# Layer 1 of a four-layer network on one core: turning onto token partitions with 128 columns of identity, and an MLP that begins with one step's statistics

## The chip, the cores and the metric

The kernel runs on one core of one Trainium2 chip. A core has a matrix engine (PE, or TensorE) with a separate path that loads its stationary operand (PEld), a vector engine (DVE), an activation engine (ACT), a general engine (POOL) and a sync engine (SP) that here issues all the data transfers. The metric is the device time of one execution in microseconds (us); lower is better. The time before is the median of three runs.

## The reference

The network works on `x` of shape 4 x 96 x 64 x 64 (batch, channels, height, width), so on 4 x 4096 = 16,384 tokens of 96 channels, in float32. Layer 0 is a two-block Mamba with a batch norm, layer 1 a ConvNeXt block, layers 2 and 3 attention-like and Fourier mixing with small quantized MLPs. The change touches layer 1 alone:

```python
def _L1_conv_ref(x, conv_w, conv_b, ln_g, ln_b, w1, b1, w2, b2, layer_scale):
    h = depthwise_conv(x, conv_w, 7 x 7, padding 3) + conv_b      # each channel by itself
    h = jnp.transpose(h, (0, 2, 3, 1))
    mu = jnp.mean(h, axis=-1, keepdims=True)                      # over the 96 channels
    var = jnp.var(h, axis=-1, keepdims=True)
    h = (h - mu) * jax.lax.rsqrt(var + LN_EPS) * ln_g + ln_b
    h = jax.nn.gelu(jnp.einsum('bhwc,cf->bhwf', h, w1) + b1, approximate=False)   # 96 -> 384
    h = jnp.einsum('bhwf,fc->bhwc', h, w2) + b2                                   # 384 -> 96
    h = jnp.transpose(h, (0, 3, 1, 2)) * layer_scale[None]
    return h + x
```

## The kernel before, in words

Layers run one after another. Layer 0 takes the first 2605 us and leaves its result in device memory (`scratch`); layer 1 is the function `layer1`; layers 2 and 3 follow. Inside layer 1, PE, DVE, ACT and POOL run their instructions in the order in which the program text issues them (`tc.manual_schedule`); the transfers on SP's queue are placed among each other by a planner, which works from its own estimate of when each is needed.

Layer 1 has three stages.

**The turn.** The tokens are cut into 16 chunks of 1024 (4 images x 4). For each chunk, `tokens` loads 96 x 1024 values of layer 0's output (`o`, 384 KB) and of the residual (`xr`, 384 KB), each with three buffers; ACT applies layer 0's batch norm to `o` (line 736), DVE adds `xr` and writes the sum into the resident tile `t` (line 737), which holds channels on the partitions. `turn` then transposes the chunk onto partitions of 128 tokens each: eight matmuls (line 744), with a block of 96 channels x 128 tokens of `t` as stationary operand and the identity as moving operand, four of them into one PSUM tile `xt_ps` of 128 x 4 x 96 (four buffers). ACT copies the first half of a chunk out (line 750), DVE the second (line 748), into the tile `xt`. In program order `tokens` of the next chunk stands ahead of `turn` of this one.

**The convolution.** With 128 tokens (two image rows) on the partitions, the 7 x 7 convolution of one channel is four matmuls with banded 128 x 128 matrices over 128 columns (lines 787 and 790). Channels go in 24 groups of 4; a group's matrices (`band`, 1 MB) are loaded with three buffers (line 761). For the fourth matmul POOL makes a copy with halves swapped (`outer`, lines 768 and 769), two groups at a time. Ahead of the ninth group, `consts2` prepares the weights of the later layers: many small loads, and a chain of small operations that ends in matmuls on PE (line 703).

**The MLP.** The 32 blocks of 512 tokens go in 8 steps of 4. Each step `k` has its statistics: `stats(k, d)` is 4 pairs of DVE operations (lines 810 and 811), and `roots(k)` turns the 16 variances into reciprocal roots by a logarithm and an exponential on ACT (lines 815 and 816). For each block `i`, `back(i)` normalizes (DVE, line 824), transposes back by identity matmuls (PE, line 829, 4 x 128 columns) and copies out (DVE, line 831); `hidden(i)` is three matmuls of 512 columns (line 838) with an exact GELU each on ACT (line 839); `out(i)` is three more matmuls (line 844) and a DVE addition into `t` (line 847). The logarithm and the exponential need other tables on ACT than the GELU, so that going over costs a table load each way. Before the first `hidden`, the kernel does the statistics and roots of steps 0 and 1 and the four `back` of step 0. After that, `back` runs four blocks ahead of `hidden`, the statistics two steps ahead, and `roots(k + 2)` stands at the end of step `k`.

A float32 matmul appears in the trace as two instruction records, each with its weight load.

Of the kernel before, what the change touches and what calls it, by code (L numbers as in the profile page):

```python
# [9 lines left out]
F32 = mybir.dt.float32  # L10
# [8 lines left out]
B, C, HW, L = 4, 96, 64, 4096  # L19
# [8 lines left out]
ACT_EXP_LN = "natural_log_exp_and_others"  # L28
# [22 lines left out]
class Net:  # L51
# [661 lines left out]
    def layer1(self, scratch, t):  # L713
        tc, nc, ins = self.tc, self.nc, self.ins
# [3 lines left out]
        with ExitStack() as ctx:  # L718
            xpool = ctx.enter_context(tc.tile_pool(name="l1x", bufs=1))
            xt = xpool.tile([128, C, B, NR + 4], F32, name="xt")  # L720
            cb = xpool.tile([128, C], F32, name="cb")
            nc.sync.dma_start(cb, ins["c_b_row"].partition_broadcast(128))
            with (
                tc.manual_schedule(engines=engines),
                tc.tile_pool(name="l1a", bufs=1) as wk,
                tc.tile_pool(name="l1ap", bufs=1, space=PSUM) as psum,
            ):
                for at in (slice(0, 2), slice(NR + 2, NR + 4)):
                    nc.gpsimd.memset(xt[:, :, :, at], 0.0)
                def tokens(b, s):  # L730
                    at = slice(b * L + s * T, b * L + (s + 1) * T)
                    o = wk.tile([C, T], F32, name="o", tag="o", bufs=3)
                    nc.sync.dma_start(o, scratch[:, at])
                    xr = wk.tile([C, T], F32, name="xr", tag="xr", bufs=3)
                    nc.sync.dma_start(xr, ins["x"][b, :, s * T : (s + 1) * T])
                    nc.scalar.activation(o, o, AF.Identity, scale=self.osc, bias=self.osh)
                    nc.vector.tensor_add(t[:, at], o, xr)

                def turn(b, s):
                    for h in range(2):  # L740
                        ps = psum.tile([128, 4, C], F32, name="xt_ps", tag="xt", bufs=4)
                        for d in range(4):
                            a = b * L + s * T + (4 * h + d) * 128
                            nc.tensor.matmul(ps[:, d], t[:, a : a + 128], self.ident[:C, :C], start=True, stop=True)
                        r = 2 + s * (T // 128) + 4 * h
                        dst = xt[:, :, b, r : r + 4].rearrange("p c r -> p r c")
                        if h:
                            nc.vector.tensor_copy(dst, ps)
                        else:
                            nc.scalar.copy(dst, ps)  # L750

                chunks = [(b, s) for b in range(B) for s in range(NSC)]
                tokens(*chunks[0])
                for k, chunk in enumerate(chunks):
                    if k + 1 < len(chunks):
                        tokens(*chunks[k + 1])
                    turn(*chunk)

                def load(g):
                    w = wk.tile([128, GC, 4, 128], F32, name="band", tag="band", bufs=3)  # L760
                    nc.sync.dma_start(w, ins["band"][g])
                    return w

                def outer(g):

                    x2 = wk.tile([128, 2 * GC, B, NR], F32, name="x2", tag="x2", bufs=3)
                    at = slice(g * 2 * GC, (g + 1) * 2 * GC)
                    nc.gpsimd.tensor_copy(x2[:64], xt[:64, at, :, 4:])
                    nc.gpsimd.tensor_copy(x2[64:], xt[64:, at, :, :NR])
                    return x2  # L770

                def small(rows, cols):
                    ps = psum.tile([128, 4, C], F32, name="w_ps", tag="xt", bufs=4)
                    return ps.rearrange("p a c -> p (a c)")[:rows, :cols]

                x2 = [outer(0)]
                for g in range(C // GC):
                    if g == 8:
                        self.consts2(wk, small)
                    if g % 2 == 0 and g + 2 < C // GC:  # L780
                        x2.append(outer(g // 2 + 1))
                    w = load(g)
                    ps = psum.tile([128, GC, B, NR], F32, name="cv_ps", tag="cv", bufs=4)
                    for d in range(GC):
                        c = g * GC + d
                        for k, j in enumerate((1, 0, 2)):
                            nc.tensor.matmul(
                                ps[:, d], w[:, d, j], xt[:, c, :, 1 + j : 1 + j + NR], start=k == 0, stop=False
                            )
                        nc.tensor.matmul(ps[:, d], w[:, d, 3], x2[g // 2][:, g % 2 * GC + d], start=False, stop=True)  # L790
                    for d in range(GC):
                        c = g * GC + d
                        dst = xt[:, c, :, 2 : 2 + NR]
                        if g % 2:
                            nc.vector.tensor_scalar_add(dst, ps[:, d], cb[:, c : c + 1])
                        else:
                            nc.scalar.activation(dst, ps[:, d], AF.Identity, bias=cb[:, c : c + 1])

            wk = ctx.enter_context(tc.tile_pool(name="l1w", bufs=1))
            psum = ctx.enter_context(tc.tile_pool(name="l1p", bufs=1, space=PSUM))  # L800
# [3 lines left out]
            def stats(k, d):  # L804
                if d == 0:
                    mv[k] = wk.tile([128, 16, 2], F32, name="mv", tag="mv", bufs=3)
                for q in range(4 * d, 4 * d + 4):
                    b, r = divmod(16 * k + q, NR)
                    st = wk.tile([128, 6], F32, name="st", tag="st", bufs=4)
                    nc.vector.bn_stats(st, xt[:, :, b, 2 + r])  # L810
                    nc.vector.bn_aggr(mv[k][:, q], st)

            def roots(k):
                rs[k] = wk.tile([128, 16], F32, name="rs", tag="rs", bufs=3)
                nc.scalar.activation(rs[k], mv[k][:, :, 1], AF.Ln, bias=self.eps)
                nc.scalar.activation(rs[k], rs[k], AF.Exp, scale=-0.5)

            def back(i):
                k, d = divmod(i, 4)
                n = wk.tile([128, 4, C], F32, name="n", tag="n", bufs=3)  # L820
                for q in range(4):
                    b, r = divmod(4 * i + q, NR)
                    at = slice(4 * d + q, 4 * d + q + 1)
                    nc.vector.tensor_scalar(  # L824
                        n[:, q], xt[:, :, b, 2 + r], mv[k][:, at, 0], rs[k][:, at], ALU.subtract, ALU.mult
                    )
                ps = psum.tile([C, 4, 128], F32, name="tp_ps", tag="tp", bufs=2)
                for q in range(4):
                    nc.tensor.matmul(ps[:, q], n[:, q], self.ident, start=True, stop=True)
                xc[i] = wk.tile([C, MB], F32, name="xc", tag="xc", bufs=7)  # L830
                nc.vector.tensor_copy(xc[i], ps.rearrange("p r n -> p (r n)"))

            def hidden(i):
                g[i] = wk.tile([128, 3, MB], F32, name="g", tag="g", bufs=3)
                n = xc.pop(i)
                for m in range(3):
                    ps = psum.tile([128, MB], F32, name="g_ps", tag="g", bufs=4)
                    nc.tensor.matmul(ps, self.c_w1[:, m * 128 : (m + 1) * 128], n, start=True, stop=True)
                    nc.scalar.activation(g[i][:, m, :], ps, AF.Gelu, bias=self.c_b1[:, m : m + 1])
# [10 lines left out]
            n = NT // MB // 4  # L850
            with tc.manual_schedule(engines=engines):
                nc.scalar.preload_act_table_set(ACT_EXP_LN)
                for k in range(2):
                    for d in range(4):
                        stats(k, d)
                    roots(k)
                for d in range(4):
                    back(d)
                for k in range(n):
                    for d in range(4):  # L860
                        hidden(4 * k + d)
                        if k + 1 < n:
                            back(4 * k + 4 + d)
                        if k + 2 < n:
                            stats(k + 2, d)
                        if d:
                            out(4 * k + d - 1)
                    if k + 2 < n:
                        nc.scalar.preload_act_table_set(ACT_EXP_LN)
                        roots(k + 2)  # L870
                    out(4 * k + 3)
# [581 lines left out]
```

## Time and profile before

| what | value |
|---|---|
| runs | 4054.6 us median (4048.88, 4054.6, 4059.62) |
| profiled execution, its own time | 4057.1 us |
| its span, first to last instruction | 4054.9 us |
| turn: first matmul to the last copy's end | 2614.7 to 2670.5 us, 55.8 us |
| convolution: to its last copy's end | to 2793.0 us, 122.4 us |
| MLP's start: to the first `hidden` matmul | to 2818.1 us, 25.2 us |
| MLP: rest of its first step | to 2843.8 us, 25.6 us |
| MLP: the other seven steps | to 3012.0 us, 168.3 us |
| layers 2 and 3 | to 4054.9 us |
| mean granted clock of PE over the span | 0.855 of full |

In the trace, a line of the timeline gives the start and length in us, the engine, the line of the kernel, the operation, the tile written and those read, the shapes, and how many such instructions are merged; in brackets, how long the engine sat idle before and what ended that. A line of the table of windows gives a stretch, its length, busy time and number of instructions for PE, PEld, DVE, ACT and POOL, then the granted share of PE's clock, the busy share of the transfer engines and the rate in GB/s.

### The profile page before, as it was taken

How to read it: one execution, taken by the hardware profiler on the slowest of the kernel's cores; microseconds unless marked ns; L12 is line 12 of the kernel's file. 1: busy time of each engine (PE TensorE's matmuls, PEld its weight loads, DVE VectorE, ACT ScalarE, POOL GpSimd, SP SyncE). 2: the span in 40 equal slices, each digit the busy share in tenths (PEclk: the TensorE clock that was granted, in tenths of full speed). 3: DMA queues.
4: the chain of work that ended last, by engine and by line, in shares of the span. 5: the costliest groups of instructions: out<-in, count | busy, mean ns of one | idle time of the engine just before them, and what ended most of it. 6: DMA issues, size and time to landing. Idle time of an engine off the chain costs nothing. (4 is left out here: it accounts for less than half of the span.)

```text
span 4054.9 us, 45522 instructions
## 1 busy us (share of the span) xinstructions
PE 3311.5 (82%) x14174; PEld 1426.9 (35%) x14174; DVE 3193.0 (79%) x2772; ACT 2423.0 (60%) x4644; POOL 2946.8 (73%) x1571
## 2 busy tenths in 40 slices
PE   6888888888888777888888887678999887887987
PEld 3222222222222222222222221376446345556642
DVE  5999999999999999999999999724632763443649
ACT  4666667666667666666766665322445665544547
POOL 2999999999999999999999999511010455333428
PEclk8788878888878888887888887668999998889989
DMA  7667567666756666675675666363000000001111
GB/s 182 144 158 172 136 150 169 158 148 163 175 130 167 168 148 160 158 171 135 162 173 141 160 165 159 103 189 136 0 1 1 1 6 3 27 27 30 45 43 54
DMA packets 183291, 468.13 MB, mean 115 GB/s; under 512 B 53236, under 2 KB 55166, under 8 KB 179968
## 3 DMA queue, kind: packets, MB, share of 16 engines
q1 hardware_dynamic: 183048, 465.21, 46.1%
q8 instruction: 113, 1.85, 0.2%
q14 instruction: 130, 1.06, 0.1%
HBM read 391.53 MB, written 73.50 MB: 115 GB/s over the span
## 5 line engine op out<-in xcount | busy, mean ns | idle before, releaser
L496 POOL TENSOR_TENSOR hs<-hs,crep 128x1024 f32<-128x1024 f32 x768 | 1797.1, 2363 | 28.8 <-DVE hs L490 24.0
L454 PE MATMUL rep<-dbl,sel_b 32*128 32x512 f32 x1152 | 403.8, 777 | 467.8 <-DVE hs L490 441.3
L474 POOL TENSOR_TENSOR up<-udb,brep 128x1024 f32<-128x1024 f32 x256 | 604.5, 2361 | 8.5 <-DMA brep<-cd 8.5
L468 ACT ACTIVATE da<-ddb,nega 128x1024 f32<-128x1024 f32 x512 | 584.8, 1149 | 13.5 <-DVE hs L490 6.9
L468 ACT ACTIVATE dap<-ddb,nega 128x1024 f32<-128x1024 f32 x256 | 286.3, 1118 | 419.9 <-DVE hs L490 417.9
L515 PE MATMUL y<-hs,sel_r 128*32 128x512 f32 x3072 | 477.9, 693 | 4.9 <-POOL hs L496 4.9
L490 DVE TENSOR_TENSOR_SCAN hs<-da,state,rep 128x1024 f32<-128x1024 f32 x192 | 450.9, 2348 | 16.7
L490 DVE TENSOR_TENSOR_SCAN hs<-da,state,u 128x1024 f32<-128x1024 f32 x192 | 450.9, 2348 | 11.2 <-DVE u L486 1.4
L490 DVE TENSOR_TENSOR_SCAN hs<-dap,state,up 128x1024 f32<-128x1024 f32 x192 | 447.2, 2329 | 6.4 <-ACT dap L468 6.0
L210 PE MATMUL ps<-n,w_x 97*64 97x512 f32 x1536 | 376.1, 633 | 6.9 <-ACT n L323 5.4
L454 PEld LDWEIGHTS rep<-dbl,sel_b 32*128 32x128 f32 x1152 | 108.4, 216 | 766.9 <-issue 519.3
L486 DVE TENSOR_TENSOR u<-udb,rep 128x1024 f32<-128x1024 f32 x256 | 314.7, 1229 | 46.2 <-PE rep L454 15.0
L486 DVE TENSOR_TENSOR rep<-udb,rep 128x1024 f32<-128x1024 f32 x256 | 310.8, 1214 | 0.3
L1038 POOL CAST hq<-y 128x512 fp8e5<-128x512 f16 x192 | 117.7, 638 | 222.3 <-issue 136.6
L210 PEld LDWEIGHTS ps<-n,w_x 97*64 97x64 f32 x1536 | 110.6, 143 | 261.5 <-issue 215.7
L1186 POOL TENSOR_TENSOR av<-av,ec 128x780 f32<-128x780 f32 x32 | 58.8, 1837 | 197.2 <-ACT av L1183 191.8
L515 PEld LDWEIGHTS y<-hs,sel_r 128*32 128x32 f32 x3072 | 65.7, 116 | 358.0 <-issue 190.0
L382 POOL TENSOR_TENSOR du<-delta,xc 128x512 f32<-128x512 f32 x96 | 122.8, 1279 | 66.0 <-DMA gp_x<-in_x 51.2
L224 PE MATMUL ps<-xc,xproj 64*102 64x512 f32 x384 | 160.9, 1001 | 3.5 <-ACT xc L344 3.5
L911 POOL MEMSET h<- 1x4096 f32 x1 | 3.5, 3506 | 212.4 <-DVE n L824 212.4
L358 ACT COPY dbl<-ps 102x512 f32<-102x512 f32 x64 | 34.4, 589 | 205.7 <-PE ps L224 205.7
L490 DVE TENSOR_TENSOR_SCAN hs<-da,rep 128x1024 f32<-128x1024 f32 x64 | 146.5, 2289 | 5.4
(256 smaller groups left out, 6573.1 us busy)
## 6 DMA issues: line engine op xcount, KB each, us to landing
ddb<-dd SPq DMA_DIRECT2D x768, 128.0 KB, 3.6
udb<-ud SPq DMA_DIRECT2D x768, 128.0 KB, 4.4
crep<-cd SPq DMA_DIRECT2D x512, 128.0 KB, 4.3
brep<-cd SPq DMA_DIRECT2D x256, 128.0 KB, 3.4
dd<-delta SPq DMA_DIRECT2D x64, 384.0 KB, 4.9
ud<-du SPq DMA_DIRECT2D x192, 128.0 KB, 2.4
band<-in_band SPq DMA_DIRECT2D x24, 1024.0 KB, 5.8
gt<-in_idft SPq DMA_DIRECT2D x64, 256.0 KB, 2.8
```

Source lines behind the costliest of these rows:

```text
L210: nc.tensor.matmul(ps[rows], w[:, 64 * p : 64 * p + 64], rhs[:, at.start + shift : at.stop + shift], start=k == 0, stop=k == len(ws) - 1, ...
L224: nc.tensor.matmul(ps, w[rows, p], x[rows, p], start=start and p == 0, stop=p == 2)
L382: nc.gpsimd.tensor_mul(u, m["delta"][:, of], m["xc"][:, of])
L454: nc.tensor.matmul(x[:, at], sel_b[rows, order[t][1]], made[k]["dbl"][rows, at], start=True, stop=True)
L468: nc.scalar.activation(da, made[k]["dd", h, j], AF.Exp, scale=nega[:, col : col + 1])
L474: nc.gpsimd.tensor_mul(u, made[k]["ud", h, j], made[k]["brep", g])
L486: nc.vector.tensor_mul(u, made[k]["ud", h, j], x)
L490: nc.vector.tensor_tensor_scan(hs[:, 1:], made[k].pop(("da", t)), u, 0.0 if s == 0 else st, ALU.mult, ALU.add)
L496: nc.gpsimd.tensor_mul(hs[:, :T], hs[:, 1:], made[k]["crep", order[t][1]])
L515: nc.tensor.matmul(made[k]["y", p][row : row + 32], sel_r, made[k]["hs", t][:, at], start=False, stop=True, skip_group_check=True,)
L1038: nc.gpsimd.tensor_copy(q[:, m, :], y2, saturate=False)
L1186: nc.gpsimd.tensor_add(v[:, 2:4], v[:, 0:2], ec)
```

## The change

The turn's identity is used with all of its 128 columns where it had 96. The PSUM tile becomes 128 x 4 x 128 (a whole bank where three quarters of one were used), and the copies read 96 of each 128 columns; the added columns are zeros and nobody reads them. The tile that `consts2` takes from the same buffers gets the same shape.

The MLP's prologue is cut to the statistics and roots of step 0 and `back(0)`. The first `hidden` comes then; `back` runs two blocks ahead instead of four (after block 0 both `back(1)` and `back(2)` are issued); in step 0 the statistics of steps 1 and 2 are issued two parts to a block, and `roots(1)` with its own table load comes after `hidden(2)`. From step 1 on only the distance of `back` differs.

```diff
                 def turn(b, s):
                     for h in range(2):
-                        ps = psum.tile([128, 4, C], F32, name="xt_ps", tag="xt", bufs=4)
+                        ps = psum.tile([128, 4, 128], F32, name="xt_ps", tag="xt", bufs=4)
                         for d in range(4):
                             a = b * L + s * T + (4 * h + d) * 128
-                            nc.tensor.matmul(ps[:, d], t[:, a : a + 128], self.ident[:C, :C], start=True, stop=True)
+                            nc.tensor.matmul(ps[:, d], t[:, a : a + 128], self.ident[:C], start=True, stop=True)
...
-                            nc.vector.tensor_copy(dst, ps)
+                            nc.vector.tensor_copy(dst, ps[:, :, :C])
...
-                            nc.scalar.copy(dst, ps)
+                            nc.scalar.copy(dst, ps[:, :, :C])
...
                 nc.scalar.preload_act_table_set(ACT_EXP_LN)
-                for k in range(2):
-                    for d in range(4):
-                        stats(k, d)
-                    roots(k)
                 for d in range(4):
-                    back(d)
+                    stats(0, d)
+                roots(0)
+                back(0)
                 for k in range(n):
                     for d in range(4):
-                        hidden(4 * k + d)
-                        if k + 1 < n:
-                            back(4 * k + 4 + d)
-                        if k + 2 < n:
+                        i = 4 * k + d
+                        hidden(i)
+                        if k == 0 and d == 2:
+                            nc.scalar.preload_act_table_set(ACT_EXP_LN)
+                            roots(1)
+                        for i2 in (1, 2) if i == 0 else (i + 2,):
+                            if i2 < 4 * n:
+                                back(i2)
+
+                        if k == 0:
+                            for d2 in (2 * (d % 2), 2 * (d % 2) + 1):
+                                stats(1 + d // 2, d2)
+                        elif k + 2 < n:
                             stats(k + 2, d)
                         if d:
-                            out(4 * k + d - 1)
+                            out(i - 1)
                     if k + 2 < n:
                         nc.scalar.preload_act_table_set(ACT_EXP_LN)
                         roots(k + 2)
```

In the built program the planner also moves five small loads of `consts2` on SP's queue ahead of one `band` load each; all other orders outside the lines shown are the same.

More of the change, by code (lines that the diff above doesn't have):

```diff
@@ L772, in small @@
                 def small(rows, cols):
-                    ps = psum.tile([128, 4, C], F32, name="w_ps", tag="xt", bufs=4)
+                    ps = psum.tile([128, 4, 128], F32, name="w_ps", tag="xt", bufs=4)
                     return ps.rearrange("p a c -> p (a c)")[:rows, :cols]
```

## The prediction

> **What bounds the kernel now.** I first read the page for where PE's clock is low, then the windows of layer 1, then its timeline. In the page's 40 slices (101 us each), the clock row falls to 6 in two slices, from 2534 to 2737 us (layer 0's end, then layer 1's turn and half its convolution), though PE is busy there in 6 or 7 tenths:
>
> ```profile
> PE   6888888888888777888888887678999887887987
> ...
> PEclk8788878888878888887888887668999998889989
> ```
>
> The windows (stretch and length; busy us and instructions of PE, PEld, DVE, ACT, POOL; clock; DMA share; GB/s) show the turn, the convolution's start, and other places where the clock rises:
>
> ```profile
> 2615.26:2618.67 3.41, 3.41 (x18) 3.41 (x17) 1.38 (x2) 2.46 (x3) 0.00 (x0) 0.50 1.03 269
> 2625.50:2628.91 3.41, 3.41 (x18) 3.41 (x17) 1.85 (x3) 1.83 (x2) 0.00 (x0) 0.50 1.04 272
> 2673.29:2676.70 3.41, 3.41 (x18) 3.41 (x18) 0.00 (x0) 0.00 (x0) 3.27 (x4) 0.50 0.00 0
> 2676.70:2680.11 3.41, 3.41 (x32) 3.41 (x32) 0.00 (x0) 1.14 (x4) 0.43 (x1) 1.00 0.37 79
> 2816.65:2820.06 3.41, 3.41 (x11) 2.38 (x11) 2.04 (x7) 0.00 (x0) 0.00 (x0) 0.50 0.01 2
> 3219.42:3222.83 3.41, 3.41 (x6) 1.28 (x5) 3.31 (x6) 2.58 (x5) 2.36 (x3) 0.50 0.00 0
> ```
>
> The turn runs at half clock for all of its 55 us with PE busy throughout: 256 records in 54.9 us, 214 ns each, so 16 to a window (the count of 18 has those that reach over its edges). The convolution, 128 columns a record, has the same 16 at half clock, and one window later 32, 107 ns each, at full. So 214 ns is what 128 columns take at half clock. The turn's 96 columns need three quarters of it, 160 ns; in the other quarter the array waits for the next 128-column weight load. Columns move in 75% of a turn window and in 100% of the convolution's, and after the latter the clock is full. The last row holds only 96 x 96 operands, moves 512 columns a record, and is followed by full clock too: what counts is moving columns, not how much of the array is filled.
>
> What ends each chunk in the turn shows in the timeline:
>
> ```profile
> 2616.51 1.22 DVE L737 TENSOR_TENSOR t<-o,xr 96x1024 f32<-96x1024 f32 x1 [1.82 <-DMA xr<-in_x]
> 2619.51 1.22 DVE L737 TENSOR_TENSOR t<-o,xr 96x1024 f32<-96x1024 f32 x1 [0.20 <-DMA xr<-in_x]
> ...
> 2630.45 0.80 ACT L750 COPY xt<-xt_ps 128x384 f32<-128x384 f32 x1 [1.58 <-PE xt_ps L744]
> 2633.87 0.80 ACT L750 COPY xt<-xt_ps 128x384 f32<-128x384 f32 x1 [1.58 <-PE xt_ps L744]
> ...
> 2669.71 0.80 DVE L748 COPY xt<-xt_ps 128x384 f32<-128x384 f32 x1 [2.61 <-PE xt_ps L744]
> ```
>
> At first the loads set the pace (3.0 us a chunk), then PE (3.42 us). ACT and DVE have about 2.0 us of work a chunk (1.23 + 0.80 and 1.20 + 0.80).
>
> The MLP's start is a chain through DVE and ACT:
>
> ```profile
> 2799.72 0.18 DVE L811 BATCH_NORM_AGGREGATE mv<-st 128x2 f32<-128x6 f32 x1
> ...
> 2802.97 0.22 ACT L816 ACTIVATE rs<-rs 128x16 f32<-128x16 f32 x1
> ...
> 2806.56 1.14 DVE L824 TENSOR_SCALAR n<-xt,mv,rs 128x96 f32<-128x96 f32 x4
> 2807.03 1.99 PE L829 MATMUL tp_ps<-ident,n 128*96 128x128 f32 x8 [15.30 <-DVE n L824]
> 2818.14 3.70 PE L838 MATMUL g_ps<-xc,c_w 96*128 96x512 f32 x6
> 2843.77 2.74 PE L838 MATMUL g_ps<-xc,c_w 96*128 96x512 f32 x6
> ```
>
> DVE begins at 2793.06; the first `hidden` is 25.08 us later, the fifth at 50.71. From 2843.77 PE is busy 167.0 of 168.3 us: the MLP is PE's.
>
> **What the Trainium skill says.** "TensorE: Matmul & The Clock Gate", Part 1: the clock is half by default and is set per free-running window of about 3413 ns from PE's activity; the trace's changes lie on such a grid (2734.73 - 2676.70 = 17 x 3.413). The same page, "LDWEIGHTS": a load's time goes with its columns, which fits 128-column loads holding 96-column matmuls to a 214 ns slot. Its Part 4 ("PE-mode transpose") says transpose-mode matmuls don't count for the clock in the same way; these are ordinary matmuls with an identity, and in the window at 2816.65 identity matmuls (line 829) fill 1.3 of the 3.41 us that raised the clock. "ScalarE: Activation LUTs", "What ACT_TABLE_LOAD costs": 1283 ns; the trace has 1.28 us.
>
> **Part 1, the turn.** 128 columns fill the slot: nothing is added at half clock (16 x 214 ns = 3.42 us a chunk, as now), and columns move 100% of the time. PE has work without a break from 2614.74 (chunk 1 is ready at 2617.73, chunk 0 done at 2618.15), so the first whole window ends within 3.4 to 6.8 us and the clock goes full. Then a chunk is 16 x 107 = 1.71 us on PE and the loads set the pace: 786 KB at the 269 to 272 GB/s of the windows is 2.90 us. PE then moves columns in 59% of the time, and in at least half of any window; counted from the records of the later layers, windows at full clock with 53% or more all kept it, those under 37% lost it, and between most kept it. So it stays. Three buffers still keep over a chunk and a half in flight (a buffer is freed 1.3 us after its chunk lands). From the addition at 2619.51 (chunk 2), the last one (chunk 15) starts 13 x 2.90 = 37.7 us later, at 2657.2; add 1.2 (addition), 1.8 (PE), 0.86 (copy): 2661.0. Now it is 2670.51. Gain 9.5 (8 to 11).
>
> The convolution's first group takes 7.06 us now (2670.61 to 2677.67), at half clock. At full clock its first fourth matmul waits for POOL's two copies (1.03 + 1.04 us), then 26 records x 0.112 = 2.9 us: 5.0. Gain 2.0, or nothing if the wait for POOL and for the last copy (together 2.5 us idle) empties a window and drops the clock; I take 2.0. The `band` loads ran at up to 418 GB/s, 2.5 us each, and the first lands some 1.5 us before it is needed. The five small loads that pass one `band` each (36 to 144 KB) hold it up by at most 0.4 us, and a group has over 7 us of cover from its load's issue: no new wait.
>
> The stall of PE before group 9 (25.8 us, up to line 703) is a chain of loads after line 680's, issued 2696.11. It moves with the convolution. The five loads moved on SP's queue may free line 680 up to 1.4 us sooner, which it waits for a `band` now: gain 0.5 (0 to 1.4). After the stall the half-clock time (4.0 us now) is redrawn: 0 (-1.4 to 0.3).
>
> **Part 2, the MLP's start,** from DVE's first statistics. Statistics and roots of step 0 end at 10.13 as now (2803.19); `back(0)` takes 3.2 (as 2806.56 to 2809.75), and `hidden(0)` starts at 13.45 in place of 25.08, with the GELU table loaded meanwhile. Call this S. Then, in PE's order with 0.88 per `back` and 2.57 per three 512-column matmuls at full clock:
> - `hidden(0)` at half clock 5.1, `back(1)` 0.9: S + 6.0.
> - `back(2)` waits for DVE's copy of 1 and its own n (1.25): S + 8.1; `hidden(1)`: S + 10.7.
> - `back(3)` stands on DVE behind eight pairs of statistics (8 x 0.42 = 3.4): starts S + 12.75, idle 2.05. `back(3)`, `out(0)`, `hidden(2)`: S + 18.8.
> - `back(4)` needs `roots(1)`, which on ACT stands behind the last GELU (S + 19.7), then 1.28 + 0.31 + 0.22: starts S + 22.05, idle 3.3; queued behind it on PE are `out(1)` and `hidden(3)`. This idle stretch empties a window in four of five positions of the grid: 1.7 to 3 us at half clock, I take 2.0.
> - `back(4)`, `out(1)`, `hidden(3)`, `back(5)`, `out(2)`, `out(3)`: 12.1; the fifth `hidden` at S + 36.2, so at 49.7 against 50.71.
> Two `back` (1.76 us of PE) and a wait of 0.4 in step 1 are still to come, which the kernel before had done: 51.8 against 50.71. Loss 1.1 (gain 1.3 to loss 4). Table loads: five up to the GELUs that follow `roots(1)`, before and after. POOL's memset (line 911), which follows the last `back`, comes 12 us later, but ends 11 us before its neighbours at 3012: nothing.
>
> **The sum:** 9.5 + 2.0 + 0.5 - 1.1 = 10.9 us. On the profiled execution that is 4057.1 - 10.9 = 4046.2; it lay 2.5 us above the median of the runs. On the median: 4043.7. A difference of 0.3% (12.2 us) is about what a measurement of this kernel can tell from no change, and the forecast lies just inside.
>
> **Rivals.**
> - The clock stays full where I let it fall, the loads go a little faster (2.8 us a chunk) and line 680 comes 1.4 sooner: 11 + 2 + 1.4 + 1 = 15.4 us, 4039. For: the saturated rate at times reached 283 GB/s. Against: the 3.3 us of idle time is nearly a whole window. 0.24.
> - Half gain: the clock falls at the convolution's start and again after the 2.05 idle, and the loads hold 3.0 us: 8 - 0 + 0 - 3 = 5 us, 4050. 0.15.
> - The change does not do what it says: the turn stays at half clock, because 96 rows or an identity count for less. Then the turn is as now and the MLP's loss remains: 4056. Against: the windows at 3219 and 2816. 0.05.
> - Slower: the MLP's first step is broken up by its three waits and stays at half clock throughout. Its 25 us of PE work would double: the fifth `hidden` at about 13.5 + 50 + 4.5 = 68 against 50.7, a loss of 19 with the two later `back`; with the 12 gained: 4062. It decides against the change from a half-clock stretch of about 25 us on. Against: `hidden(0)` and `back(1)` alone are 6 us without a break. 0.05.
>
> The forecast has 0.51. Its own range is 4039 to 4048, as the grid's position falls, and somewhat under half of it lies past 0.3%: faster 0.22 of it, and nearly all of the first rival (0.22): 0.44. Slower by over 0.3% is a part of the last rival and a bad draw in the later layers: 0.04. The rest, 0.52, is within. For 8 in 10 the range has to take in the first rival's faster side and the half gain: 4035 to 4053.
>
> **What would show it.** Right: clock 1.00 in the turn from its second or third window on, DVE's addition ended by `xr`'s load and 2.9 us apart, the last copy near 2661; the first `hidden` 13.5 us after the first statistics; PE waiting about 3 us for `rs` at `back(4)`. Wrong: 0.50 through the turn; chunks under 2.7 or over 3.2 us apart; the stall before line 703 grown by what the turn won; clock 0.50 past the MLP's first step.

## The result, and the profile after

The changed kernel takes 4045.6 us (median of 20 runs, 4037.2 to 4052.4) against 4055.5 for the kernel before, which also ran 20 times. The ratio is 0.9972, with a 95% interval of 0.9966 to 0.9979: 11.4 us faster (8.5 to 13.8; the difference of the two medians is 9.9). The forecast was 10.9 us. The sum came out nearly right; its largest term did not.

The two profiled executions, stage by stage (from the span's start, each stage from the end of the one above):

| stage | before | after | change | forecast |
|---|---|---|---|---|
| up to the turn's first matmul | 2614.7 | 2612.1 | -2.6 | untouched |
| turn, to the end of its last copy | 55.8 | 51.4 | -4.4 | -9.5 |
| convolution, to the first statistics | 122.6 | 118.1 | -4.4 | -2.5 |
| MLP, to the end of its last addition | 219.7 | 220.5 | +0.8 | +1.1 |
| the rest | 1042.2 | 1043.6 | +1.5 | untouched |
| span | 4054.9 | 4045.7 | -9.2 | -10.9 |

First the page's 40 slices of the changed kernel, the same two rows as before:

```profile
PE   7888888888888778888778887668999888787887
...
PEclk7888878888878888887888887788999998989979
```

The two slices that stood at 6 before are 7 and 8 now (the 26th and the 27th figure of the clock row). Next the windows of the changed kernel (stretch, length; busy us and instructions of PE, PEld, DVE, ACT, POOL; clock; DMA share; GB/s), on the clock's own grid:

```profile
2612.62:2616.03 3.41, 3.41 (x18) 3.41 (x17) 1.33 (x2) 2.23 (x3) 0.00 (x0) 0.50 1.03 240
2616.03:2619.44 3.41, 2.64 (x23) 2.45 (x22) 2.66 (x3) 2.09 (x3) 0.00 (x0) 1.00 1.03 244
2636.51:2639.92 3.41, 1.94 (x17) 1.75 (x17) 1.95 (x2) 1.82 (x3) 0.00 (x0) 1.00 1.05 246
2639.92:2643.33 3.41, 2.54 (x12) 2.24 (x12) 1.94 (x2) 1.88 (x2) 0.00 (x0) 0.50 1.02 241
2817.42:2820.83 3.41, 3.14 (x10) 2.38 (x11) 2.00 (x8) 1.03 (x1) 0.00 (x0) 0.50 0.01 2
```

The turn's first matmul is at 2612.10, and after one whole window of it the clock is 1.00, as forecast. But the loads move 240 to 246 GB/s in these windows and not 269 to 272, with the DMA engines saturated (share 1.02 to 1.05). The third row shows the consequence: PE now has so little to do in a window (1.94 of 3.41 us) that it loses the clock again, for two windows. That should cost next to nothing, because PE at half clock needs 3.42 us a chunk and the loads 3.2. The timeline of the turn shows the pace:

```profile
2617.29 1.22 DVE L737 TENSOR_TENSOR t<-o,xr 96x1024 f32<-96x1024 f32 x1 [0.55 <-DMA xr<-in_x]
2620.57 1.22 DVE L737 TENSOR_TENSOR t<-o,xr 96x1024 f32<-96x1024 f32 x1 [1.34 <-DMA xr<-in_x]
2623.82 1.22 DVE L737 TENSOR_TENSOR t<-o,xr 96x1024 f32<-96x1024 f32 x1 [1.31 <-DMA xr<-in_x]
...
2662.69 0.80 DVE L748 COPY xt<-xt_ps 128x384 f32<-128x384 f32 x1 [1.43 <-PE xt_ps L744]
```

Each addition waits for `xr`'s load, as forecast, but they are 3.23 us apart on average, not 2.90. The convolution's first group runs from the first matmul of line 787 to that of the second group. These two lines, and the stall before line 703, in the kernel before:

```profile
2670.61 1.62 PE L787 MATMUL cv_ps<-xt,band 128*128 128x128 f32 x6 [0.94 <-issue]
...
2677.67 0.83 PE L787 MATMUL cv_ps<-xt,band 128*128 128x128 f32 x6
...
2730.02 0.93 PE L703 MATMUL w_ps<-bn_d,a_w2raw 96*96 96x96 f32 x4 [25.84 <-DVE bn_d L699]
```

The PE timeline of the same places and of the MLP's first step, in the changed kernel:

```profile
2663.59 0.91 PE L787 MATMUL cv_ps<-xt,band 128*128 128x128 f32 x6 [0.94 <-ACT xt L750]
...
2668.82 0.84 PE L787 MATMUL cv_ps<-xt,band 128*128 128x128 f32 x6
...
2719.98 0.92 PE L703 MATMUL w_ps<-bn_d,a_w2raw 96*96 96x96 f32 x4 [24.57 <-DVE bn_d L699]
...
2795.03 5.47 PE L838 MATMUL g_ps<-xc,c_w 96*128 96x512 f32 x6 [0.78 <-DVE xc L831]
2800.31 1.06 PE L829 MATMUL tp_ps<-ident,n 128*96 128x128 f32 x8
2802.51 1.19 PE L829 MATMUL tp_ps<-ident,n 128*96 128x128 f32 x8 [1.14 <-DVE n L824]
...
2808.21 1.19 PE L829 MATMUL tp_ps<-ident,n 128*96 128x128 f32 x8 [1.94 <-DVE n L824]
...
2817.69 1.99 PE L829 MATMUL tp_ps<-ident,n 128*96 128x128 f32 x8 [3.13 <-DVE n L824]
...
2831.33 2.74 PE L838 MATMUL g_ps<-xc,c_w 96*128 96x512 f32 x6
```

The MLP's statistics begin at 2781.61. The first `hidden` comes 13.42 us later (forecast 13.45), the idle times before `back(2)`, `back(3)` and `back(4)` are 1.14, 1.94 and 3.13 us (forecast 1.25, 2.05, 3.3), one half-clock window follows the last of them, and the fifth `hidden` comes 49.72 us after the first statistics (forecast 49.7).

### The profile page after: what moved, and what is told of

Its sections match the earlier page's. It is cut to its first block, busy times and chain, and to the rows that moved or that the text cites. A ratio compares the mean times of both kernels' runs of the same rounds, so it can differ in the third digit from the quotient of the medians.

```text
span 4045.7 us, 45519 instructions
## 1 busy us (share of the span) xinstructions
PE 3295.7 (81%) x14174; PEld 1405.4 (35%) x14174; DVE 3193.8 (79%) x2772; ACT 2423.2 (60%) x4644; POOL 2947.1 (73%) x1571
## 5 line engine op out<-in xcount | busy, mean ns | idle before, releaser
L210 PE MATMUL ps<-n,w_x 97*64 97x512 f32 x1536 | 367.9, 622 | 8.7 <-ACT n L323 5.0
```

What stands on the lines that cost most here:

```text
L210: nc.tensor.matmul(ps[rows], w[:, 64 * p : 64 * p + 64], rhs[:, at.start + shift : at.stop + shift], start=k == 0, stop=k == len(ws) - 1, ...
```

## The experiments

Four questions: which part carries the gain, why the warm turn (the one at full clock) ran at 3.2 us a chunk, how many columns the clock needs, and what the waits cost that the change leaves.

**Each part alone.** `turn_only` is the kernel before with the four edited lines of the turn and `small`; `mlp_only` is the changed kernel with these put back:

```diff
-ps = psum.tile([128, 4, 128], F32, name="xt_ps", tag="xt", bufs=4)
-nc.tensor.matmul(ps[:, d], t[:, a : a + 128], self.ident[:C], start=True, stop=True)
+ps = psum.tile([128, 4, C], F32, name="xt_ps", tag="xt", bufs=4)
+nc.tensor.matmul(ps[:, d], t[:, a : a + 128], self.ident[:C, :C], start=True, stop=True)
...
```

The lines left out are the two copies and `small`.

> The kernel before with the 128 columns of identity alone. Theory (the turn and the convolution carry the whole gain): the trace of after shows 4.4 us won in the turn, 4.4 in the convolution, 0.8 lost in the MLP, so this kernel should be 8 to 10 us faster than before and 0 to 2 us faster than the whole change. Clock 1.00 from the second or third window of the turn. Rival (the MLP's start carries part of the gain): 6 us faster or less. On the pace of the loads: if full-speed matmuls slow them, a chunk takes 3.2 us again; if the pace differs from one execution to the next, it may be 2.9.

> The whole change with the turn's 96 columns put back: the new order at the MLP's start alone. Theory: 0.3 to 1.7 us slower than before, and in its trace the fifth hidden about 1 us sooner after the first statistics than before, the MLP's end 0.8 later. Rival (the new order is worth something): 2 us faster or more. The turn is at half clock throughout, so PE sets 3.42 us a chunk; where the loads are saturated at its start, they move 270 GB/s if full-speed matmuls were what slowed them in after, and may move 245 if not.

`turn_only` took 4051.0 us against 4057.1, ratio 0.9978 (0.9969 to 0.9987): 8.9 us faster (5.3 to 12.6). `mlp_only` had a ratio of 0.9994 (0.9987 to 1.0001): between 5.3 us faster and 0.4 slower, where 0.3 to 1.7 slower was expected. Its trace shows the expected MLP (first `hidden` at 13.42, the stage 220.1 us, 0.4 longer than before), and nothing in that stage that would make the kernel faster. So the turn carries most of the gain, and the MLP's own share is too small for the runs to give it a size: the interval of `turn_only` just reaches the 6 us of the rival, and whether it beats the whole change, as expected, can't be told from intervals that overlap.

The turn of `turn_only`, in its timeline, is the one that had been forecast:

```profile
2631.09 1.22 DVE L737 TENSOR_TENSOR t<-o,xr 96x1024 f32<-96x1024 f32 x1 [0.94 <-DMA xr<-in_x]
2633.94 1.22 DVE L737 TENSOR_TENSOR t<-o,xr 96x1024 f32<-96x1024 f32 x1 [0.90 <-DMA xr<-in_x]
2637.02 1.22 DVE L737 TENSOR_TENSOR t<-o,xr 96x1024 f32<-96x1024 f32 x1 [1.14 <-DMA xr<-in_x]
2639.90 1.22 DVE L737 TENSOR_TENSOR t<-o,xr 96x1024 f32<-96x1024 f32 x1 [0.93 <-DMA xr<-in_x]
```

It has 2.93 us a chunk on average, 46.8 us from first matmul to last copy, and 274 GB/s, from the same instructions of the turn as in the changed kernel. And `mlp_only`, whose matmuls are at half clock, moves 242 to 251 GB/s where its loads are saturated. So full-speed matmuls are not what slows the loads.

**Once more the same kernel.** `after_again` is the changed kernel unchanged.

> The whole change once more, for another execution of its turn. If the pace of the loads is the execution's, the chunk takes anything from 2.85 to 3.3 us; if the new order of the MLP (and with it the order of the loads) made it slower than in turn_only, it takes 3.2 again.

It took 4046.8 us; its chunks start at 2.95 to 2.97 us and end at 3.2, 3.12 on average, in one turn. So the pace varies with the execution: 3.23 and 3.12 us for the same kernel, and 2.95 to 3.2 within one turn. The chip may have a part in it: the profiles of one chip (`after_again`, `outs_first`, `early_loads`) lie at 3.09 to 3.26, and of another (`combined`, and `contig` below) at 2.92 to 2.94. But the chip of `turn_only`, with 274 GB/s, is also that of `mlp_only`, with 242 to 251. In the six profiles with a warm turn of this form the average chunk was 2.93 (`turn_only`), 2.94 (`combined`, below), 3.09 (`outs_first`, below), 3.12, 3.23 and 3.26 (`early_loads`, below), and the turn 46.8 to 51.8 us long, 49.3 on average; in the four with half-clock turns 55.8. A turn gains 4.0 to 9.0 us, 6.5 on average. In all six the clock rose 3.9 to 6.7 us after the first matmul. The two slowest, 3.23 and 3.26 us, lost it for two windows on the way; the others kept it.

**How many columns.** `cols112` and `cols120` are the changed kernel with 112 and 120 columns:

```diff
-ps = psum.tile([128, 4, 128], F32, name="xt_ps", tag="xt", bufs=4)
-nc.tensor.matmul(ps[:, d], t[:, a : a + 128], self.ident[:C], start=True, stop=True)
+ps = psum.tile([128, 4, 120], F32, name="xt_ps", tag="xt", bufs=4)
+nc.tensor.matmul(ps[:, d], t[:, a : a + 128], self.ident[:C, :120], start=True, stop=True)
```

> The whole change with 112 columns of identity: columns move in 112/128 = 87.5% of the turn's half-clock time, between 75% (stayed at half clock for 55 us) and 100% (rose). If any share well over 75% is enough, the clock rises after a window or two and the time is that of the whole change (4045). If it takes nearly all of a window (more than nine tenths), the clock stays at 0.50 through the turn, chunks are 3.42 us, and the time is about 4053 to 4055.

> The whole change with 120 columns of identity: columns move in 93.75% of the turn's half-clock time, between 112 columns (87.5%, stayed at half clock for the whole turn) and 128 (rose after the first whole window). If nine tenths of a window are enough, the clock rises by the third window and the chunk takes 2.9 to 3.3 us; if the window must be full, the clock stays at 0.50 and the chunk takes 3.42 us.

Windows of `cols112`, then of `cols120`, in mid-turn:

```profile
2634.66:2638.07 3.41, 3.41 (x18) 3.41 (x18) 1.85 (x2) 1.83 (x3) 0.00 (x0) 0.50 1.04 249
```

```profile
2634.66:2638.07 3.41, 3.41 (x18) 3.41 (x18) 1.85 (x3) 1.83 (x3) 0.00 (x0) 0.50 1.03 247
```

Both stayed at 0.50 to the end of the turn, with 3.41 us a chunk once PE set the pace (single runs: 4052.9 and 4044.1 us; the kernel before ran in 4044.8 us beside the latter). PE counts as busy for the whole window in all of them. So in this turn 120 columns, which move in 94% of the time, are not enough, and 128 are.

The share of moving columns alone does not decide, however. Two successive windows of `mlp_only` at the start of its convolution, then two of `outs_first` (below) at the start of its turn:

```profile
2671.58:2675.00 3.42, 2.87 (x13) 2.87 (x14) 0.00 (x0) 0.00 (x0) 3.26 (x4) 0.50 0.00 0
2675.00:2678.41 3.41, 3.41 (x33) 3.41 (x32) 0.00 (x0) 1.14 (x4) 1.38 (x2) 1.00 0.29 38
```

```profile
2612.94:2616.36 3.42, 3.33 (x15) 3.33 (x16) 1.26 (x2) 2.06 (x2) 0.00 (x0) 0.50 1.03 244
2616.36:2619.77 3.41, 3.41 (x18) 3.41 (x17) 2.04 (x2) 2.27 (x3) 0.00 (x0) 0.50 1.04 253
```

In the first window PE is at work for 84% of the time, and the clock is full after it (in `combined`, below, the window from 2676.20 is the same). In the third it is at work for 97%, and the clock stays at half. What differs is the height of the stationary operand: 128 partitions in the convolution, 96 in the turn. Multiplied by that height, as a part of 128, the first share is still 0.84 at most, the third is at most 0.73, `cols120` has 0.70, and a whole window with 128 columns in the turn has 0.75. I counted the windows of all fourteen profiles from 2605 us on that hold float32 matmuls only, with stationary operands of 96 or 128 columns. (A record's 128 columns count as 107 ns at full clock and 214 at half.) The best single limit on the moving columns puts 34 of 649 half-clock windows on the wrong side, and 39 of 3796 at full clock; on columns times partitions, 10 and 4, with limits near 0.74 and 0.36. This is a reading made after the fact that fits the traces. No run here changed the partitions of the matmuls and nothing else.

**Half of the bytes.** `half_bytes` drops the turn's loads of `x`:

```diff
-xr = wk.tile([C, T], F32, name="xr", tag="xr", bufs=3)
-nc.sync.dma_start(xr, ins["x"][b, :, s * T : (s + 1) * T])
-nc.vector.tensor_add(t[:, at], o, xr)
+nc.vector.tensor_add(t[:, at], o, o)
```

> The whole change without the turn's loads of x: the addition takes o twice, so the residual is left out and the values differ; same instructions on every engine, half of the bytes. Theory (the loads set the pace of the warm turn): 393 KB at 245 GB/s is 1.6 us a chunk, so ACT and DVE become the limit at 2.05 to 2.2 us, the turn ends some 15 us sooner than in after, and the time is about 4030. Rival (PE or the chain of addition, matmul and copy sets 3.2 us): no change, 4045.

The time was as expected (4029.8 us), but not for the reason given. The turn took 44.5 us, 6.9 less than in the changed kernel, at 1.8 to 4.2 us a chunk: the planner put band loads and those of `consts2` among the turn's on SP's queue, so the bytes that were left out were partly replaced, and PE was at half clock from 2635.5 to 2645.7. The other 8.5 us came from the convolution: with `bn_rows` issued at 2650.6, during the turn, PE's stall before line 703 was 10.1 us instead of 24.6. That pointed to the last experiments of this section.

**Longer rows, nearer rows, more partitions.** `rows8k` loads two chunks at once (rows of 8192 bytes, two buffers; `x2` has two buffers for room). `contig` reads one contiguous stretch for each load, so that the tokens land in wrong places, and `to128` spreads the same bytes over 128 partitions (rows of 3072 bytes). The core of `rows8k`, of `contig` and of `to128`:

```diff
+o2 = wk.tile([C, 2, T], F32, name="o", tag="o", bufs=2)
+nc.sync.dma_start(o2, scratch[:, two].rearrange("c (k t) -> c k t", k=2))
...
-nc.sync.dma_start(o, scratch[:, at])
+nc.sync.dma_start(o, scratch[6 * k : 6 * k + 6].rearrange("r (q t) -> (r q) t", t=T))
...
+nc.sync.dma_start(
+    o[:, :768], scratch[6 * k : 6 * k + 6].rearrange("r (q t) -> r q t", t=T).rearrange("r q t -> (r q t)").rearrange("(p w) -> p w", w=768)
+)
```

> The whole change, with the turn's loads made for two chunks at once: rows of 8192 bytes in place of 4096, two buffers in place of three (and two for x2). Theory (the size of the rows sets the pace, as the band's 8 KB rows at 410 GB/s suggest): the chunk goes from 2.9 to 3.2 us down to about 2.5 (two buffers: half of 3.8 + 2 + 4.1 us for two chunks), 7 to 11 us won in the turn. Rival (these tensors are read at 240 to 270 GB/s whatever the row): 2.9 to 3.3 us a chunk again, 0 to 2 us lost by the fewer buffers.

> The whole change, but the turn's two loads of a chunk each read one contiguous stretch of 393216 bytes (six rows of scratch, 24 rows of x) in place of 96 rows of 4096 bytes that lie 65536 and 16384 bytes apart; the same 96 partitions, packets and instructions. The tokens come out in the wrong places, so the values differ. Theory A (the distance of the rows in memory makes the packets slow): packets fall from 250 to 280 ns towards 160 ns, the loads are no longer the limit, and a chunk takes about 2.05 to 2.3 us (ACT and DVE). Theory B (where they are written, 96 partitions on 16 DMA engines, makes them slow): 245 to 280 ns and 2.9 to 3.3 us again.

> As contig, and the same 393216 bytes go to 128 partitions of 3072 bytes each (the addition then works on the first 96 partitions, with 256 stale columns, so the values differ). Theory B: 128 partitions at the bands' rate, about 400 GB/s, so a chunk takes 2.05 to 2.3 us. Theory A, if contig has already shown it: the same 2.05 to 2.3 us as contig. If both stay at 2.9 to 3.3 us, neither the distance of the rows nor the partitions set the pace.

Windows of the same 6 us in `after`, `rows8k`, `contig` and `to128`, in this order:

```profile
2634.00:2640.00 6.00, 3.75 (x30) 3.56 (x31) 3.39 (x4) 3.31 (x4) 0.00 (x0) 0.99 1.04 245
```

```profile
2634.00:2640.00 6.00, 4.45 (x38) 4.07 (x36) 3.82 (x4) 3.66 (x5) 0.00 (x0) 1.00 1.02 242
```

```profile
2634.00:2640.00 6.00, 3.99 (x23) 3.51 (x22) 3.92 (x4) 4.07 (x5) 0.00 (x0) 0.78 1.03 270
```

```profile
2634.00:2640.00 6.00, 5.02 (x41) 4.55 (x40) 5.08 (x6) 4.94 (x6) 0.00 (x0) 1.00 0.94 317
```

Doubling the rows changed nothing: 242 GB/s, packets of 8192 bytes at 511 to 566 ns through most of the turn, 3.10 us a chunk; the kernel's ratio to before was 0.9982 (0.9972 to 0.9991). Neither did the distance of the rows matter: packets at 248 to 259 ns and 2.92 us a chunk, within what the kernel has anyway. 128 partitions did: 317 GB/s in this window, 313 from 2620 to 2650, and 2.46 us a chunk, though not the 400 GB/s that were expected (single runs: `contig` 4046.7, `to128` 4034.5 us; in both the planner also moved the loads of `consts2` ahead of later bands, so these times hold more than the turn). So part of why these loads are slow is that they go to 96 partitions. What makes one execution move 245 and another 274 GB/s stays open; it is not the speed of PE, and neither longer nor nearer rows brought more than that.

**The waits in the MLP's first step.** `outs_first` splits `out` into its matmuls and its addition, and puts the matmuls ahead of `back` on PE in the first step:

```diff
+ps = out(i - 1) if k == 0 and d else None
 for i2 in (1, 2) if i == 0 else (i + 2,):
     if i2 < 4 * n:
         back(i2)
...
-out(i - 1)
+add(i - 1, ps if k == 0 else out(i - 1))
```

> The whole change, with out's matmuls put ahead of back's on PE in the MLP's first step (the additions stay where they were). Theory (the idle 1.9 us before back(3), 3.1 us before back(4) and the half-clock window after the latter are what the new order costs): out fills them, both waits fall below 1 us, no half-clock window near the fifth hidden, and the MLP from first statistics to last addition takes 4 to 6 us less than after's 220.5 us. Rival (something else sets the first step's pace, such as ACT or DVE): under 2 us less.

The PE timeline of `outs_first`, from its second `hidden` on:

```profile
2803.88 2.74 PE L838 MATMUL g_ps<-xc,c_w 96*128 96x512 f32 x6
2806.46 2.74 PE L844 MATMUL m_ps<-g,c_w 128*96 128x512 f32 x6
2809.04 1.04 PE L829 MATMUL tp_ps<-ident,n 128*96 128x128 f32 x8
...
2815.79 1.17 PE L829 MATMUL tp_ps<-ident,n 128*96 128x128 f32 x8 [0.56 <-DVE n L824]
```

`back(3)` follows without a wait, `back(4)` waits 0.56 us in place of 3.13, the clock stays full, and the MLP takes 215.5 us, 5.0 less than in the changed kernel (4038.3 us in its one run). So the two waits and the half-clock window were the price of the new order, and the order of `out` pays it back.

**The stall before line 703.** `early_loads` issues the loads that `consts2` needs behind the third band, and leaves its arithmetic in group 8:

```diff
 w = load(g)
+if g == 2:
+    raw = self.loads2(wk)
...
-self.consts2(wk, small)
+self.consts2(wk, small, *raw)
```

> The whole change, and the twelve loads of consts2 that its work in group 8 waits for are issued behind the first three band loads, with two buffers each for w1raw and w2raw; its arithmetic stays in group 8. Theory (the idle stretch of PE before line 703 is the loads' chain, held behind bands on SP's queue): the 24.6 us idle go down to the arithmetic of DVE and ACT, 2 to 6 us, so the time is some 18 to 22 us below the whole change, about 4026; the clock may stay full across it (another 1 to 4). Rival (the loads come early and hold up the bands, bn_rows taking 20 us on few engines): new idle time of 5 to 15 us in the first groups, and only 5 to 10 us won.

It took 4044.6 us, ratio 0.9972 (0.9965 to 0.9979), as the whole change without it. The idle time is the rival's, and less was won than even the rival allowed (5 to 10 us). Idle time in its PE timeline:

```profile
2692.92 1.65 PE L804 MATMUL cv_ps<-xt,band 128*128 128x128 f32 x6 [13.66 <-DMA band<-in_band]
2722.46 0.93 PE L718 MATMUL w_ps<-bn_d,a_w2raw 96*96 96x96 f32 x4 [8.27 <-DVE bn_d L714]
```

13.7 + 8.3 us stand in place of 24.6: the same stall in another place. Why the bands were late shows in the DMA view of `early_loads` from 2650 to 2722, in 40 slices of 1.8 us:

```profile
GB/s 241 253 250 248 266 309 391 419 430 255 72 32 26 26 24 35 147 235 29 50 139 378 393 423 423 163 11 23 259 392 309 382 296 314 259 291 273 282 23 0
```

For about six slices, from 2668, only 24 to 72 GB/s move. In that time lie `bn_rows`' 97 packets of 3072 bytes, 127 ns each: 97 x 127 ns is 12.3 us, and the first starts 12.0 us before the last ends. They went one after another (in the changed kernel too: 97 x 149 ns = 14.4, in 14.1 us). The Trainium skill says this: "DMA: Bandwidth & Descriptors", section "Why a DMA increments its semaphore by 16 and not by 1", has a load use the largest number of engines up to 16 that divides the counts of both sides' outermost dimensions; 97 is prime, so one. The trace agrees.

**A version with all of it.** `combined` adds to the change `outs_first`, the early loads, the cut of the 97-partition loads, and a later place for `a_w2`:

```diff
-nc.sync.dma_start(rows, ins["bn1_rows"].partition_broadcast(C + 1))
+for at in (slice(0, C), slice(C, C + 1)):
+    nc.sync.dma_start(rows[at], ins["bn1_rows"].partition_broadcast(at.stop - at.start))
...
-self.consts2(wk, small, *raw)
+last = self.consts2(wk, small, *raw)
+if g == 12:
+    last()
```

> A version that should beat both: the whole change, outs_first, and early_loads with the three loads of 97 partitions cut into 96 and 1 (their packets went one after another, 97 x 149 ns = 14.4 us for bn_rows, and the bands stood behind them), and a_w2's two matmuls moved from group 8 to group 12. Theory: the idle 24.6 us before line 703 are gone, no band is late, the half-clock stretch after it (2 us) is gone, and the MLP's 5 us as in outs_first: 28 to 32 us below the whole change, about 4016. Rival (bands are late all the same, since all those loads, 1.3 MB, stand between the third band and the fourth; or DVE's and ACT's work on the constants holds up the convolution's additions): PE idle 5 to 12 us in the first twelve groups, 4025 or more.

It took 4021.2 us against 4057.2, ratio 0.9911 (0.9895 to 0.9928): 36 us faster than the kernel before (29 to 43), and some 25 faster than the change, by the two ratios, where 28 to 32 was expected. Two waits over half a microsecond for anything are left in its convolution once the second group has begun, and here is its DMA view from 2648 to 2720:

```profile
2676.74 1.65 PE L815 MATMUL cv_ps<-xt,band 128*128 128x128 f32 x6 [2.96 <-DMA band<-in_band]
2708.40 0.91 PE L815 MATMUL cv_ps<-xt,band 128*128 128x128 f32 x6 [0.74 <-DMA band<-in_band]
```

```profile
GB/s 259 257 257 257 269 414 423 423 310 206 42 221 214 135 370 269 396 423 294 131 432 273 419 219 414 200 369 182 432 118 319 237 328 259 364 178 191 396 132 410
```

The long trough is gone (`bn_rows`' 97 packets are through in 4.5 us, beside other loads; of the edits only the cut bears on them), and the convolution takes 96.0 us in place of 118.1. The MLP has 215.2. One late band of 3 us remains, in the direction of the rival.

## Why the prediction was right, and where it was not

- **The clock in the turn**: right in what was forecast. It rose after the first whole window in each of the six warm turns, and the columns that were added are the cause: with 96, 112 and 120 of 128 it stayed at half, with 128 it rose. The rule behind it, "what counts is moving columns, not how much of the array is filled", is not borne out: the convolution's windows above rose with fewer moving columns. The window at 3219, on which the rule rested, could not tell: with 96 partitions and columns moving throughout, it too has 0.75 on the count by columns times partitions. On that count the change had almost nothing to spare, which the prediction did not see: that 128 columns were enough on 96 partitions was partly luck.
- **"786 KB at the 269 to 272 GB/s of the windows is 2.90 us", and the gain of 9.5 (8 to 11) from it**: this step failed. I read one rate off one execution and took it for the hardware's. The term measured 4.4 us in the profiled execution (3.23 us a chunk), and 4.0 to 9.0, 6.5 on average, over six. With 3.2 us a chunk, "in at least half of any window" and "So it stays" on the clock failed too (columns moved in some 47% of the window that lost it, at 107 ns for each 128), and cost nothing that can be told from the rest.
- **The convolution's first group, gain 2.0**: 7.06 us went to 5.23, a gain of 1.8. The doubt that went with it came true elsewhere: in two of the six warm turns (`early_loads`, `outs_first`) the clock fell here, and the group took 6.87 and 6.57 us. Over the six the gain is 1.3.
- **The stall, gain 0.5 (0 to 1.4)**: 25.84 to 24.57, a gain of 1.3 in these two profiles; over four with a warm turn and four with a half-clock one (24.57, 24.87, 24.77, 25.19 against 25.84, 25.36, 25.67, 25.46) it is 0.7. That the five moved loads are its reason is not shown. The further 1.2 us of the convolution are two late bands that the profile of before has after the stall (1.2 us of PE's wait for `band` between 2735 and 2792) and that of after has not.
- **The MLP, loss 1.1**: 0.8, with each wait within 0.2 us of its forecast. `outs_first` shows what the waits cost, 5 us. The loss itself can't be told from none: the old order took 219.7 us (before) and 220.8 (`turn_only`) in its two profiles, and the new one 220.0 to 223.9 in other executions, as the clock's windows fall.
- **Why the sum held all the same**: partly by luck. The turn gave about 5 us less in the profile, and the convolution about 2 more; the span's remaining difference is in stages that the change doesn't touch, which moved by -2.6 and +1.5 us. Against the runs, with the averages over the profiles: 6.5 + 1.3 + 0.7 - 0.8 = 7.7 us, a little below the 8.5 to 13.8 that they show. Between 1 and 6 us of the measured gain are therefore not accounted for by the traces, which have one execution each.
- **The rivals**: the half gain came nearest in the turn (3.0 us a chunk was its figure, and the clock did fall on the way), but not in the time. The turn did not stay at half clock, and the MLP's first step did not stay cold.

## What to carry to other kernels

A stream's saturated rate, read from one execution, is one draw: look at a second execution, or at the same stream elsewhere in the trace, before a forecast rests on it, and put the spread into the range. Before a matmul is made faster, look at whether the clock will follow: compare its moving columns, and the partitions of its stationary operand, with windows of the same trace after which the clock rose. PE's busy time doesn't tell that. When a wait for a load is moved earlier, look at what stands behind that load on the DMA engines: the load that makes a stall can make the same stall for whatever follows it.

## What was not expected of the hardware

- With 120 moving columns to a load of 128, the clock stayed at 0.50 for the whole turn of 55.8 us, though PE was busy in every window; with 128 it rose after the first whole window, at most 6.7 us after the first matmul.
- Windows of the convolution, on 128 partitions, brought full clock with PE at work for 84% of them; windows of the turn, on 96 partitions, did not with 94 or 97%.
- At full clock, a window with 1.94 us of PE work in 3.41 lost the clock, with no wait of PE longer than 1.5 us around it.
- The same loads to 96 partitions, saturated, moved 245 GB/s in one execution and 274 in another; to 128 partitions 313 to 317, while the band's went at up to 426.
- A load to 97 partitions put its packets one after another: 97 packets of 3072 bytes took 12 to 14 us, and in `early_loads` PE waited 13.7 us for a band that was issued after it.
